# Cross attention on one core: the output product in units of 512 columns

## The chip, the core and the metric

The kernel runs on one core of one Trainium2 chip. The metric is the time of one execution on the device in microseconds, as the median of several runs. A profiled execution gives, beside its own time, the trace from which all durations here come. Engines are named as the profile names them: PE (TensorE, matmuls), PEld (its weight loads, which overlap the matmuls), DVE (VectorE), ACT (ScalarE), POOL (GpSimd) and SP (SyncE, which here only issues DMAs).

## What is computed

Thirty-two batches of 512 tokens with 640 channels attend, in 20 heads of 32 channels, to 77 keys of their own batch. The other branches of the reference see empty slices here (the context has just 77 rows), so what is left is:

```python
q = heads(x @ to_q_w)                       # x: (32, 512, 640) f32
k = heads(ctx @ to_k_w)                     # ctx: (32, 77, 1024) f32
v = heads(ctx @ to_v_w)
p = softmax(q @ k.T / sqrt(32))
out = merge(p @ v) @ to_out_w + to_out_b + x
```

All tensors are f32.

## The kernel before

**Precision.** Each f32 operand of a product is split into a high and a low part, which ACT (a cast, the high part), DVE or POOL (a subtraction, the low part) make. A product is then three matmuls: high x high, high x low, low x high (`PAIRS`).

**Stages.** A prologue makes keys and values of all batches and stores them in scratch memory. Then come 32 batches. A batch is five stages `j`, each for 128 of the 640 channels, that is four heads. A stage of number n = 5b + j has: the query product of the next stage (`queries`, L481, 15 matmuls of 512 columns into the one bank `pq`), the scores (`score_tile`, L516, four token tiles of 308 and twice 154 columns into three banks `sc`), their maximum (L527, DVE), exponentials (L541, ACT), normalisation (L556, POOL), a block transpose of the probabilities (L562, DVE) and their way through scratch memory (`pd` stores L571, `raw` loads L586 and L588, SP's queue), which turns them so that keys lie on partitions. Four stages later (`LAG`) come the value product (`value_pass`, L632, six matmuls of 512 columns into `pa`, two banks), a copy of its lower half by ACT (L646), two additions of halves by DVE (L650), and the split into `at` (L662 ACT, L667 DVE). Low parts of the queries are made by DVE (L723), those of the probabilities by DVE (L610) and POOL (L617).

**Output product.** Once a batch's five `at` tiles are there, `project` (L685) forms the output: for each of four token tiles t and two halves h of 320 channels, 15 matmuls (5 stages x 3 pairs) with `at` held and the weights `wo_s` moved, into one of two banks `po` that take turns. `add_output` (L700, DVE) adds the bank to `xr`, a tile of 128 tokens x 640 channels that SP loaded from x (L674) and to which POOL added the bias (L678); SP stores it (L703).

**Order.** Nothing is scheduled by the program's builder. The order on every engine follows three tables of tokens: `FILL` (batches 0 and 1, with the end of the prologue), `PLAN` (each of batches 2 to 30, 29 times) and `LAST_` (batch 31 and what is left). A token such as `4p8` is a stage, an operation and an argument. Those spoken of below: `q` a fifth of a query product (three matmuls), `s` a score tile, `m` its maximum, `v` one value matmul, `p` a step of the output product (three matmuls), `g` a low query half, `z` the block transpose, `A` ACT's copy of the lower half, `a` an addition of halves, `h` and `L` the split of `at`, `f` an addition of output to `xr`, `o` its store, `ur` the load of `xr`, `b` the bias. Steps of the output product for one batch are spread over the five stages of the batches after it. The last batch's output product is in tokens of its own (`Zp`, `Zf`, `Zo`).

Of the kernel before, what the change touches and what calls it, by code (L numbers as in the profile page):

```python
# [8 lines left out]
F32 = mybir.dt.float32  # L9
FPR = mybir.dt.float32r  # L10
AF = mybir.ActivationFunctionType
ALU = mybir.AluOpType
# [11 lines left out]
P = 128  # L24
Q = 32
# [26 lines left out]
def kernel(  # L52
# [25 lines left out]
    nc = tc.nc  # L78
    B, S, C = x.shape
    CA = ehs.shape[2]  # L80
    NT = B * NKEY
    NQ = S // P
# [354 lines left out]
    z = main.tile([P, NBLK, NQ, Q], F32, name="z")  # L437
    for g, (j0, nj) in enumerate(GROUPS):
        vb = main.tile([P, nj, 2, 2, P], FPR, name=f"vb{g}")
        vbs.append(vb)  # L440
# [239 lines left out]
    def output_bank(b, t, h):  # L680
        pos[b, t, h] = late[1].tile([P, S], F32, tag="po", name="po", bufs=2)

    def project(b, t, h, j):
        for m, (a, c) in enumerate(PAIRS):
            nc.tensor.matmul(  # L685
                pos[b, t, h][:, :HALF],
                ats[b * NC_ + j][:, a, t * P : (t + 1) * P],
                wos[0][:, j, c, h * HALF : (h + 1) * HALF],
                start=(j == 0 and m == 0),
                stop=(j == NC_ - 1 and m == 2),  # L690
            )

    STEPS = [(0, h, j) for h in range(2) for j in range(4)] + [(0, 0, 4), (0, 1, 4)]
    STEPS += [(t, h, j) for t in range(1, NQ) for h in range(2) for j in range(NC_)]
    CUTS = (0, 4, 8, 10, 16, 20, 24, 28, 32, 36, 40)
    def add_output(b, t, h):
        xr, cols = xrs[b, t], slice(h * HALF, (h + 1) * HALF)
        nc.vector.tensor_tensor(xr[:, cols], pos.pop((b, t, h))[:, :HALF], xr[:, cols], ALU.add)  # L700
# [8 lines left out]
    RESIDUAL = {1: (1, 0), 3: (1, 1), 4: (1, 2), 0: (2, 3)}  # L709
    BIAS = {2: (1, 0), 4: (1, 1), 0: (2, 2), 1: (2, 3)}  # L710
# [14 lines left out]
    def open_late():  # L725
# [96 lines left out]
    def issue(b, token):  # L822
# [46 lines left out]
        elif op == "p":  # L869
            t, h, c = STEPS[arg[0] if len(arg) == 1 else 10 * arg[0] + arg[1]]  # L870
            if c == 0:
                output_bank(out_b, t, h)
# [151 lines left out]
```

## Time and profile before

| | before |
|---|---|
| time, median of 3 runs (us) | 1891.99 |
| lowest and highest (us) | 1890.35, 1901.48 |
| profiled execution, its own time (us) | 1896.68 |
| its span, first to last instruction (us) | 1894.9 |
| granted TensorE clock, mean | 0.996 |

In the profile, a row of a group shows line, engine, operation, what it writes and reads, shape and count, then busy time in all and mean duration of one, then idle time of the engine just before such instructions and what ended it. A row of the windows shows the stretch, its length, and busy time (with the count of instructions) of PE, PEld, DVE, ACT and POOL, then the granted clock, the busy share of the 16 DMA engines and GB/s. A row of the chain of waits or of the timeline shows start, length (in the timeline from the first start to the last end of merged instructions) and what. A row of the waits shows who waited for whom: us in all, times, the longest.

### The profile page before, as it was taken

The page shows a single profiled execution, that of the slowest core. Times are in us where ns is not written, and L with a number is a line of the kernel's source. Part 1 is how long each engine was busy: PE and PEld are TensorE (multiplying, and loading weights), DVE is VectorE, ACT ScalarE, POOL GpSimd, SP SyncE. Part 2 cuts the span into 40 slices and gives each one's busy share as a digit, 9 for nine tenths or more (in the row PEclk, how much of TensorE's full clock was granted, in tenths as well). Part 3 has the DMA queues.
Part 4 walks back from the last instruction along what each step waited for, and adds up shares of the span by engine and source line. Part 5 has one row for each costly group of instructions (what it writes and reads, how often), then busy time and mean ns, then how long its engine had stood idle before and what let it go on. Part 6 is the DMA issues. An engine that isn't in the chain of part 4 may idle for free.

```text
span 1894.9 us, 37179 instructions
## 1 busy us (share of the span) xinstructions
PE 1864.1 (98%) x10332; PEld 1660.5 (88%) x10332; DVE 1561.0 (82%) x2494; ACT 1534.6 (81%) x6210; POOL 1363.5 (72%) x1116
## 2 busy tenths in 40 slices
PE   9999998999999999999999999999999999999998
PEld 7888896799989898899899998998899899998997
DVE  5445346999989898999999998999998999998985
ACT  3232247999989899999999998999999999998984
POOL 1100067888878888888888888888888888887874
PEclk9999999999999999999999999999999999999999
DMA  9888868989989889898999999889989899988876
GB/s 186 195 196 246 201 178 230 225 239 239 233 223 236 235 234 234 231 233 236 239 228 238 243 237 235 232 234 236 238 239 237 234 234 241 235 237 228 228 201 201
DMA packets 565020, 431.34 MB, mean 228 GB/s; under 512 B 191120, under 2 KB 473168, under 8 KB 564816
## 3 DMA queue, kind: packets, MB, share of 16 engines
q1 hardware_dynamic: 559760, 413.62, 85.2%
q0 software_dynamic: 4416, 14.34, 2.3%
q8 instruction: 85, 1.39, 0.3%
q14 instruction: 119, 0.97, 0.2%
q10 hardware_dynamic: 640, 1.02, 0.2%
HBM read 247.17 MB, written 181.64 MB: 226 GB/s over the span
## 4 chain that ended last, share of the span: by engine, by line
PE 63%; DMA 13%; SPq 5%; POOL 5%; ACT 5%; DVE 5%; issue 3%; POOLq 0%; DVEq 0%; ACTq 0%
PE pq L481 19%; PE po L685 18%; PE pa L632 7%; PE sc L516 7%; PE pv L191 6%; PE pk L191 6%; DMA raw<-pd 5%; DMA pd<-z 3%; ACT pn L541 2%; SPq L571 2%; DMA xs<-in_x_dram 2%; POOL kb L458 1%; DMA out_dram<-xr 1%; POOL xr L678 1%; DVE z L562 1%
## 5 line engine op out<-in xcount | busy, mean ns | idle before, releaser
L541 ACT ACTIVATE pn<-sc,nm 128x77 f32<-128x77 f32 x2560 | 801.1, 352 | 27.5 <-DVE nm L527 20.1
L685 PE MATMUL po<-wo_s,at 128*128 128x320 f32 x3840 | 685.9, 311 | 0.7 <-DVE at L667 0.2
L685 PEld LDWEIGHTS po<-wo_s,at 128*128 128x128 f32 x3840 | 612.8, 188 | 44.2 <-DVE xr L700 1.1
L481 PE MATMUL pq<-xt,wq_s 128*128 128x512 f32 x2400 | 627.9, 397 | 2.4 <-DVE qt L723 2.3
L541 ACT ACTIVATION_READ_ACCUMULATOR pn<-sc,nm 128x1 f32 x2560 | 587.5, 231 | 0.0
L481 PEld LDWEIGHTS pq<-xt,wq_s 128*128 128x128 f32 x2400 | 428.8, 189 | 71.5 <-issue 1.6
L556 POOL TENSOR_TENSOR pn<-pn,rs 128x1232 f32<-128x1232 f32 x160 | 388.9, 2431 | 44.5 <-DVE rs L551 42.6
L516 PEld LDWEIGHTS sc<-kb,qt 128*128 128x128 f32 x1920 | 298.7, 189 | 44.1 <-ACT pn L541 16.2
L527 DVE TENSOR_REDUCE nm<-sc 128x4 f32<-128x308 f32 x640 | 292.2, 465 | 34.5 <-PE sc L516 30.7
L516 PE MATMUL sc<-kb,qt 128*128 128x154 f32 (+1 forms) x1920 | 300.9, 277 | 14.8 <-ACT pn L541 9.6
L632 PE MATMUL pa<-pp,vb 128*128 128x512 f32 x960 | 308.9, 404 | 6.0 <-DVE at L667 4.6
L617 POOL TENSOR_TENSOR pp<-raw,pp 64x512 fp32r<-64x512 f32 x160 | 223.4, 1396 | 97.7 <-ACT pp L599 66.8
L650 DVE TENSOR_TENSOR pa<-pa,aw 64x512 f32<-64x512 f32 x320 | 222.6, 695 | 36.5 <-ACT aw L646 29.2
L562 DVE STREAM_TRANSPOSE z<-pn 128x1280 f32<-128x1280 f32 x160 | 241.6, 1510 | 12.2 <-DMA pd<-z 2.9
L719 POOL CAST qt<-qt 64x512 fp32r<-64x512 f32 x320 | 195.7, 612 | 59.3 <-ACT qt L715 45.7
L292 POOL TENSOR_TENSOR xt<-xs,xt 128x512 fp32r<-128x512 f32 x160 | 202.9, 1295 | 43.0 <-ACT xt L288 39.8
L723 DVE TENSOR_TENSOR qt<-pq,qt 64x512 fp32r<-64x512 f32 x320 | 217.4, 680 | 12.7 <-ACT qt L715 8.0
L678 POOL TENSOR_TENSOR xr<-xr,bias 128x640 f32<-128x640 f32 x128 | 202.4, 1582 | 26.8 <-DMA xr<-in_x_dram 12.3
L610 DVE TENSOR_TENSOR pp<-raw,pp 128x1024 fp32r<-128x1024 f32 x160 | 200.1, 1250 | 18.3 <-ACT pp L601 17.9
L632 PEld LDWEIGHTS pa<-pp,vb 128*128 128x128 f32 x960 | 170.4, 190 | 26.9 <-issue 4.7
L646 ACT COPY aw<-pa 64x1024 f32<-64x1024 f32 x160 | 162.2, 1014 | 31.6 <-PE pa L632 28.9
L601 ACT CAST pp<-raw 128x1024 fp32r<-128x1024 f32 x160 | 168.0, 1050 | 20.4 <-DMA raw<-pd 20.1
(48 smaller groups left out, 1617.6 us busy)
## 6 DMA issues: line engine op xcount, KB each, us to landing
pd<-z SPq DMA_DIRECT2D x640, 160.0 KB, 3.3
raw<-pd SPq DMA_DIRECT2D x160, 512.0 KB, 4.5
xs<-in_x_dram SPq DMA_DIRECT2D x128, 320.0 KB, 5.8
xr<-in_x_dram SPq DMA_DIRECT2D x128, 320.0 KB, 4.2
out_dram<-xr SPq DMA_DIRECT2D x127, 320.0 KB, 4.2
raw<-pd SPq DMA_DIRECT2D x160, 128.0 KB, 4.4
v_dram<-vs SPq DMA_DIRECT2D x80, 192.0 KB, 4.0
k_dram<-ks POOLq DMA_DIRECT2D x20, 512.0 KB, 4.5
```

The lines of the kernel that those rows point to most:

```text
L191: nc.tensor.matmul(held[j][:, :gn], w[:, k, a, :], cts[g, k][:, c, :gn], start=(k == 0 and n == 0), stop=(k == NK - 1 and n == 2),)
L481: nc.tensor.matmul(pqs[n], wq_s[:, k, a, j * P : (j + 1) * P], xts[b, k][:, c, :], start=(k == 0 and m == 0), stop=(k == NC_ - 1 and m == 2),)
L516: nc.tensor.matmul(sc[:, cols], qt[:, m, t * P : (t + 1) * P], keys_, start=(m == 0), stop=(m == 2),)
L527: nc.vector.tensor_reduce(nm, sc[:, :KCOLS].rearrange("p (h k) -> p h k", k=NKEY), AX.X, ALU.max, negate=True)
L541: nc.scalar.activation(pnb[n % 2][:, at, :NKEY], sc[:, i * NKEY : (i + 1) * NKEY], AF.Exp, bias=nm[:, i : i + 1], accum_out=sms[n][:, at : ...
L556: nc.gpsimd.tensor_tensor(pf, pf, rs.unsqueeze(2).to_broadcast([P, NQ * HPC, NKEY]), ALU.mult)
L562: nc.vector.transpose(z.rearrange("p b t j -> p t b j"), pn.rearrange("p (t h) k -> p t (h k)", t=NQ).rearrange("p t (b i) -> p t b i", i=Q),)
L617: nc.gpsimd.tensor_tensor(pp[64:, 4, :], raw[:64, 2, :], pp[:64, 4, :].bitcast(F32), ALU.subtract)
L632: nc.tensor.matmul(pas[n][:, p, :], vb[:, p, t, :], pp[:, c, :], start=(c == p), stop=(c == p + 2),)
L650: nc.vector.tensor_tensor(pa[64 * p : 64 * p + 64, 0], pa[:64, p], aw[:, p], ALU.add)
L678: nc.gpsimd.tensor_tensor(xrs[b, t], xrs[b, t], bias, ALU.add)
L685: nc.tensor.matmul(pos[b, t, h][:, :HALF], ats[b * NC_ + j][:, a, t * P : (t + 1) * P], wos[0][:, j, c, h * HALF : (h + 1) * HALF], start= ...
```

## The change

The output product of batches 0 to 30 is cut into five units of 512 columns in place of eight of 320. Units 1 to 4 are token tiles: `at` held, the first 512 channels of the weights moved, one full bank. Unit 0 is the last 128 channels for all 512 tokens, with the weights held and `at` moved, so its result has channels on partitions and tokens along the row. Sixteen transposes by DVE (`turn_output`, token `y`), each of 32 partitions x 128 elements, turn it from the bank into a tile `zt` in SBUF, from where POOL adds it to `xr` (`add_turned`, token `U`). The first 512 channels are added by DVE as before (`add_output`, token `f`). The last batch keeps the old form (`project_half`, `add_half`). The steps are numbered anew (`STEPS`), loads of `xr` and bias additions go to other stages, and all three order tables are replaced.

```diff
+    zt = main.tile([P, NQ, P], F32, name="zt")
...
-    def output_bank(b, t, h):
-        pos[b, t, h] = late[1].tile([P, S], F32, tag="po", name="po", bufs=2)
-
-    def project(b, t, h, j):
+    def output_bank(b, u):
+        pos[b, u] = late[1].tile([P, S], F32, tag="po", name="po", bufs=2)
+
+    WIDE = C - P
+
+    def project(b, u, j):
+
+        at, w = ats[b * NC_ + j], wos[0][:, j]
+        for m, (a, c) in enumerate(PAIRS):
+            if u == 0:
+                held, moved = w[:, a, WIDE:], at[:, c, :]
+            else:
+                held, moved = at[:, a, (u - 1) * P : u * P], w[:, c, :WIDE]
+            nc.tensor.matmul(
+                pos[b, u], held, moved, start=(j == 0 and m == 0), stop=(j == NC_ - 1 and m == 2)
+            )
+
+    def project_half(b, t, h, j):
...
-    STEPS = [(0, h, j) for h in range(2) for j in range(4)] + [(0, 0, 4), (0, 1, 4)]
-    STEPS += [(t, h, j) for t in range(1, NQ) for h in range(2) for j in range(NC_)]
-    CUTS = (0, 4, 8, 10, 16, 20, 24, 28, 32, 36, 40)
-    def add_output(b, t, h):
+    def turn_output(b, q, a):
+        src = pos[b, 0][q * Q : (q + 1) * Q].rearrange("p (t a j) -> p t a j", t=NQ, j=Q)
+        nc.vector.transpose(zt[a * Q : (a + 1) * Q, :, q * Q : (q + 1) * Q], src[:, :, a, :])
+
+    def add_turned(b, t):
+        xr = xrs[b, t]
+        nc.gpsimd.tensor_tensor(xr[:, WIDE:], xr[:, WIDE:], zt[:, t, :], ALU.add)
+
+    def add_output(b, t):
+        xr = xrs[b, t]
+        nc.vector.tensor_tensor(xr[:, :WIDE], pos.pop((b, 1 + t)), xr[:, :WIDE], ALU.add)
+
+
+    STEPS = [(0, j) for j in range(4)] + [(1, 0), (0, 4)] + [(1, j) for j in range(1, NC_)]
+    STEPS += [(u, j) for u in range(2, NQ + 1) for j in range(NC_)]
+
+    def add_half(b, t, h):
         xr, cols = xrs[b, t], slice(h * HALF, (h + 1) * HALF)
-        nc.vector.tensor_tensor(xr[:, cols], pos.pop((b, t, h))[:, :HALF], xr[:, cols], ALU.add)
+        nc.vector.tensor_tensor(xr[:, cols], pos.pop((b, (t, h)))[:, :HALF], xr[:, cols], ALU.add)
...
     PIECES = {3: (1, 0), 4: (1, 2), 0: (2, 4), 1: (2, 6), 2: (2, 8)}
-    RESIDUAL = {1: (1, 0), 3: (1, 1), 4: (1, 2), 0: (2, 3)}
-    BIAS = {2: (1, 0), 4: (1, 1), 0: (2, 2), 1: (2, 3)}
+    RESIDUAL = {3: (1, 0), 4: (1, 1), 0: (2, 2), 1: (2, 3)}
+    BIAS = {4: (1, 0), 0: (2, 1), 1: (2, 2), 2: (2, 3)}
...
     PLAN = (
-        "0q0 0c1 0q1 0c0 0q2 0R 0h 0l 0q3 0uk130 0q4 0L 0d0 0s0 0d1 0Q 0s1 0m0 0ux3 0p16 0r 0e0 0f10 0v0 "
...
+        "0q0 0q1 0q2 0q3 0c1 0b1 0q4 0uk130 0s0 1uv15 0p10 0r 0h 0m0 0d0 0R 0c0 0s1 0d1 0s2 0e0 0l "
...
+        "3w2 4l 4p5 3w1 4q3 4y03 4ur1 4e1 4y10 4q4 4y32 4ux0 4y20 4y00 4ux1 4K01 4v1 4y01 4Q 4p7 4y02 "
+        "4ux2 4N 4y33 4e2 4g0 4s3 4v3 4y23 4v0 4v5 4g1 4v2 4p8 4y12 4y13 4p9 4k1 4m3 4z 4k0 4v4 4A 4b0 "
+        "4w2 4e3 4a1 4w3 4y11 4K00 4w0 4y31 4y21 4y30 4w1 4y22 4a0 "
     ).split()
...
-    ADDED = {4: 1, 0: 2, 1: 2, 2: 2, 3: 2}
+    ADDED = {0: 2, 1: 2, 2: 2, 3: 2}
...
+        elif op == "y":
+            turn_output(out_b, *arg)
+        elif op == "U":
+            add_turned(b - ADDED[j], *arg)
```

More of the change, by code (lines that the diff above doesn't have):

```diff
@@ L678, in add_bias @@
         nc.gpsimd.tensor_tensor(xrs[b, t], xrs[b, t], bias, ALU.add)
-    def output_bank(b, t, h):
-        pos[b, t, h] = late[1].tile([P, S], F32, tag="po", name="po", bufs=2)
-    def project(b, t, h, j):
+    def output_bank(b, u):
[12 more added lines that the diff above has]
+    def project_half(b, t, h, j):
         for m, (a, c) in enumerate(PAIRS):
             nc.tensor.matmul(
-                pos[b, t, h][:, :HALF],
+                pos[b, (t, h)][:, :HALF],
                 ats[b * NC_ + j][:, a, t * P : (t + 1) * P],
@@ L869, in issue @@
         elif op == "p":
-            t, h, c = STEPS[arg[0] if len(arg) == 1 else 10 * arg[0] + arg[1]]
+            u, c = STEPS[arg[0] if len(arg) == 1 else 10 * arg[0] + arg[1]]
             if c == 0:
-                output_bank(out_b, t, h)
-            project(out_b, t, h, c)
+                output_bank(out_b, u)
+            project(out_b, u, c)
+        elif op == "y":
+            turn_output(out_b, *arg)
+        elif op == "U":
+            add_turned(b - ADDED[j], *arg)
         elif op == "f":
@@ L952, in final @@
                 if i < 3:
-                    pos[last, t, h] = ps.tile([P, S], F32, tag="sc", name="po", bufs=3)
+                    pos[last, (t, h)] = ps.tile([P, S], F32, tag="sc", name="po", bufs=3)
                 elif i == 3:
-                    pos[last, t, h] = ps.tile([P, S], F32, tag="pq", name="po", bufs=1)
+                    pos[last, (t, h)] = ps.tile([P, S], F32, tag="pq", name="po", bufs=1)
                 elif i < 6:
-                    output_bank(last, t, h)
+                    output_bank(last, (t, h))
                 else:
@@ L960, in final @@
                         pas[N] = late[1].tile([P, 2, S], F32, tag="pa", name="po", bufs=1)
-                    pos[last, t, h] = pas[N][:, i - 6]
-            project(last, t, h, j)
+                    pos[last, (t, h)] = pas[N][:, i - 6]
+            project_half(last, t, h, j)
         elif op == "f":
-            add_output(last, *arg)
+            add_half(last, *arg)
         elif op == "o":
```

150 rows, old and new, of tables (FILL, LAST_, PLAN) are left out of this document.

## Prediction

> **What bounds the kernel now.** I read the page's totals first, then the windows by stage, then the chain of waits inside one batch, then the waits of PE and DVE.
>
> ```profile
> PE 1864.1 (98%) x10332; PEld 1660.5 (88%) x10332; DVE 1561.0 (82%) x2494; ACT 1534.6 (81%) x6210; POOL 1363.5 (72%) x1116
> ```
> ```profile
> core 0: us, PE busy (x) PEld busy (x) DVE busy (x) ACT busy (x) POOL busy (x), PEclk, DMA share, GB/s
> 0.00:340.00 340.00, 324.62 (x1471) 274.18 (x1472) 172.80 (x275) 134.01 (x404) 90.45 (x106) 0.98 0.86 206
> ...
> 1002.31:1494.30 491.99, 490.60 (x2826) 442.27 (x2826) 446.91 (x716) 451.75 (x1885) 410.98 (x327) 1.00 0.90 236
> 1800.00:1895.00 95.00, 88.86 (x528) 80.29 (x527) 69.71 (x111) 61.93 (x236) 55.98 (x42) 1.00 0.68 200
> ```
> The averages of the page mix a prologue, in which DVE is half idle, with the batches. The third row is ten steady batches: 491.99 us, so 49.2 us a batch. There PE is busy 490.60, ACT 451.75 (92%) and DVE 446.91 (91%, 44.7 us a batch). PE sets the pace, but two engines follow close behind it.
>
> A busy PE is not a PE at its best, so the next view is the chain of waits through one batch, where a piece's length over its matmul count is the spacing from start to start:
>
> ```profile
> 1002.31 3.49 PE pq L481 x15
> ...
> 1007.93 0.70 PE pa L632 x3
> ...
> 1009.23 2.63 PE po L685 x18
> 1011.86 3.43 PE pq L481 x15
> 1015.29 0.69 PE sc L516 x6
> ...
> 1051.51 3.49 PE pq L481 x15
> ```
> The reader is to see two things. The same piece comes back after 1051.51 - 1002.31 = 49.20 us: one period. And spacing goes with columns: 3.43/15 to 3.49/15 = 229 to 233 ns for 512 columns, 2.63/18 = 146 ns for 320. The group rows give 311 ns for the 320-column matmul, but that counts its fill and drain, which the next one overlaps; whoever counts with durations finds a large gain that isn't there. A batch by spacings: 75 query matmuls at 231, 120 output matmuls at 146, 30 value matmuls at 233 and 20 score tiles at 0.345 us make 17.33 + 17.53 + 7.0 + 6.9 = 48.8 us. Only some 0.4 us of the 49.2 is waiting.
>
> ```profile
> PEld sc L516 <- ACT pn L541: 6.2, 12, 1.1
> PEld pa L632 <- DVE at L667: 2.5, 9, 0.3
> ```
> These are the largest waits ahead of PE between 600 and 1700 us, 22 batches: 0.4 us a batch, the same answer from the other side.
>
> **Output product on PE.** Before, 4 token tiles x 2 halves x 15 = 120 matmuls of 320 columns; after, 5 units x 15 = 75 matmuls of 512. The columns are the same, 38,400. At 146 ns the old ones take 17.53 us a batch. At 229 to 233 ns the new ones take 17.15 to 17.45, middle 17.30. Saved: 0.23 us a batch, ends 0.08 and 0.38. It applies to batches 0 to 30, as the last batch keeps its halves: 31 x 0.23 = 7 us (2.5 to 12), and it counts in full because PE is the pace. The 45 weight loads that go lay beside matmuls and give nothing more. Swapping which operand is held changes nothing in these spacings: query matmuls already hold weights and move activations.
>
> [...]
>
> **DVE.** Eight adds of 320 become four of 512, and 16 transposes of 32 x 128 from PSUM come in.
>
> ```profile
> L700 DVE TENSOR_TENSOR xr<-po,xr 128x320 f32<-128x320 f32 x256 | 120.7, 473 | 8.4 <-PE po L685 5.4 <-POOL xr L678 0.2
> L278 DVE STREAM_TRANSPOSE xs<-xs 128x640 f32<-128x640 f32 x128 | 100.0, 817 | 4.7 <-DMA xs<-in_x_dram 4.6
> L167 DVE STREAM_TRANSPOSE craw<-cs 128x512 f32<-128x512 f32 x32 | 21.6, 696 | 7.6 <-DMA cs<-in_ctx_dram 7.3
> L254 DVE STREAM_TRANSPOSE vs<-pv 128x512 f32<-128x512 f32 x20 | 14.2, 710 | 15.5 <-DMA v_dram<-vs 13.3 <-PE pv L191 2.2
> ```
> ```profile
> 1002.87 0.84 DVE L527 TENSOR_REDUCE nm<-sc 128x4 f32<-128x308 f32 x2
> ...
> 1005.84 0.24 DVE L551 RECIPROCAL rs<-sm 128x16 f32<-128x16 f32 x1
> 1006.00 1.16 DVE L610 TENSOR_TENSOR pp<-raw,pp 128x1024 fp32r<-128x1024 f32 x1
> ...
> 1026.11 1.56 DVE L278 STREAM_TRANSPOSE xs<-xs 128x640 f32<-128x640 f32 x2
> ...
> 1029.76 1.51 DVE L562 STREAM_TRANSPOSE z<-pn 128x1280 f32<-128x1280 f32 x1
> 1031.20 0.21 DVE L551 RECIPROCAL rs<-sm 128x16 f32<-128x16 f32 x1
> ...
> 1035.82 0.68 DVE L667 TENSOR_TENSOR at<-pa,at 128x512 fp32r<-128x512 f32 x1
> 1036.42 1.56 DVE L278 STREAM_TRANSPOSE xs<-xs 128x640 f32<-128x640 f32 x2
> ...
> 1043.57 0.47 DVE L700 TENSOR_TENSOR xr<-po,xr 128x320 f32<-128x320 f32 x1
> 1043.97 0.46 DVE L527 TENSOR_REDUCE nm<-sc 128x4 f32<-128x308 f32 x1
> ```
> On DVE too the next instruction starts before the last has ended, so I price by starts. An add of 320 costs 1043.97 - 1043.57 = 0.40, one of 512 costs 0.60 (the L667 row, also PSUM with SBUF): 8 x 0.40 - 4 x 0.60 = 0.8 us a batch saved. Transposes: 1.44 for 1280 (1029.76 to 1031.20), 1.56 - 0.82 = 0.74 for 640, so 1.09 ns an element, and 0.74 - 512 x 1.09 ns = 0.18 for 128. From PSUM it is 14 ns more (710 against 696). No row shows so small a transpose, and none of 32 partitions. Its lower bound is 0.16, the 16-element reciprocal (1005.84 to 1006.00); its upper one the whole duration with nothing overlapped, 710 - 384 x 1.09 = 0.29. I take 0.20, from the transposes, the nearest rows in kind: 3.2 us a batch (2.6 to 4.6). DVE goes from 44.7 to 44.7 - 0.8 + 3.2 = 47.1 us of a 49.0 us period (46.5 to 48.5). I cost this at nothing because PE still has more to do; if that cover goes, it is rival B.
>
> [...]
>
> **Where the transposes stand.** They follow step p5, which ends unit 0, in stage 4 of the table. Behind them on DVE wait the two query halves (g), a score maximum (m3), the block transpose (z) and the half adds (a1, a0). Unit 2 (p10, next batch) needs unit 0's bank, so it waits for the last transpose. From the end of p5 PE has 6 query matmuls, 9 of units 0 and 1, 6 value matmuls and a score tile (21 x 0.232 + 0.35 = 5.2 us), then 15 query matmuls and a tile (3.8): 9.0 us.
>
> ```profile
> L646 ACT COPY aw<-pa 64x1024 f32<-64x1024 f32 x160 | 162.2, 1014 | 31.6 <-PE pa L632 28.9
> ```
> DVE passes 11 transposes, g0, g1, m3 and z in 2.2 + 1.2 + 0.4 + 1.4 = 5.2 us; a1 must wait for the last value matmul and ACT's copy of 1.01, at 6.4; then a1 and the five last transposes end at 8.0. That leaves 1.0 us; at 0.29 each it is still 0.5. So p10 isn't late. The maximum m0 of the next batch needs its tile at 9.0, after a0 (8.6). ACT gets nothing new.
>
> **POOL and the queues.** The table adds four 128 x 128 additions a batch.
>
> ```profile
> L678 POOL TENSOR_TENSOR xr<-xr,bias 128x640 f32<-128x640 f32 x128 | 202.4, 1582 | 26.8 <-DMA xr<-in_x_dram 12.3 <-issue 4.6 <-DMA kb<-k_dram 2.7
> L292 POOL TENSOR_TENSOR xt<-xs,xt 128x512 fp32r<-128x512 f32 x160 | 202.9, 1295 | 43.0 <-ACT xt L288 39.8
> ```
> 1582 - 512 x 2.24 = 0.44 us each, 1.7 us a batch (nothing to 5.2, at L292's price): POOL goes from 41.1 to 42.8 of 49; nobody else gains or loses by it. The output store on SP now waits for POOL's addition too, and pd stores and raw loads stand behind it; the table puts each addition ahead of its store by a stage in three tiles, and by half a stage in the last. Residual loads move later by one or two stages, bias additions go with them; DMA bytes and issues are unchanged. All priced at nothing.
>
> **Order tables.** All three are new. In the steady part an order can win at most the 0.4 us a batch of waiting. In the prologue PE idles 340 - 324.6 = 15.4 us, much of it before any token of the table, and at the end 6.1. I take zero, plus or minus 5.
>
> **Sum.** The profiled execution took 1896.7 us for a span of 1894.9; minus 7 it is 1889.7. It stood 4.7 above the median, so the forecast against the median is 1892 - 7 = 1885.
>
> **Rivals.**
> A, PE stays the pace, 1885 (1875 to 1895).
>
> B, slower: DVE becomes the pace. For it: 47.1 of 49.0 leaves 1.9 us idle where there were 4.5, and idle here is mostly answers of other engines:
>
> ```profile
> DVE at L667 <- ACT at L662: 40.1, 51, 1.1
> DVE nm L527 <- PE sc L516: 19.2, 43, 0.6
> DVE pa L650 <- ACT aw L646: 14.2, 51, 0.7
> DVE pp L610 <- ACT pp L601: 10.3, 15, 1.7
> ```
> That is 83.8 us over 22 batches, 3.8 a batch, in loops that a longer DVE queue hides only in part. It decides once transposes and remaining idle pass 49.0 - 43.9 = 5.1 us: at 0.20 each, if over 1.9 us of idle stays. With 3.0 staying the batch is 43.9 + 3.2 + 3.0 = 50.1, +0.9 x 30 = 27 us: 1919. [...] Against it: the walk above, where each loop keeps half a microsecond.
>
> C, the new order also removes waits: 0.4 x 29 = 12 us and 5 at the ends on top of A: 1868. Against it: a fuller DVE makes waits, it doesn't remove them.
>
> D, nothing: the spacing goes strictly with columns and saves 0.08 a batch: 1890.
>
> **How the numbers follow.** A 0.55, D 0.13, C 0.08, B 0.24. One per cent, 19 us, is about what a measurement of this kernel can tell from no change: under 1873 only C lies, 0.08 faster; A and D are the same, 0.68; B is slower, 0.24. The likeliest is A: 1885. The range takes in most of C (1869) and the milder half of B (1920).
>
> **What would show it.** In the profile after: 512-column output matmuls in the chain at 229 to 233 ns; PE near 490 of 492 us in ten batches, and a period of 49.0; the transposes near 0.27 us long and 0.20 from start to start; DVE near 96%. If instead PE waits before po for a transpose, or sc and pa for DVE, and the period passes 49.6, B has it. If DVE sits under 93%, a transpose is cheaper than I think. A time under 1869 would mean that 512 columns run closer than the query matmuls do.

## The result, and the profile after

| | before | after |
|---|---|---|
| median of 20 runs (us) | 1896.01 | 1901.81 |
| lowest and highest (us) | 1888.68, 1905.08 | 1899.28, 1906.82 |
| profiled execution, its own time (us) | 1896.68 | 1900.52 |
| its span (us) | 1894.9 | 1898.7 |

The ratio of after to before is 1.0032, 95% interval 1.0018 to 1.0045. That is within the one per cent that the prediction calls the same, and 1901.8 lies inside its range. But the change lost 6 us where the forecast had it win 7: the range held the time only because it was drawn up to 1920 to take in some of rival B. The kernel before is itself 4 us slower here than in the three runs that the forecast counted from.

First the totals of the page of the kernel after:

```profile
PE 1859.1 (98%) x8937; PEld 1551.9 (82%) x8937; DVE 1666.5 (88%) x2866; ACT 1526.2 (80%) x6210; POOL 1387.1 (73%) x1240
```

Then the windows, 600 to 1600 us, of before and of after:

```profile
core 0: us, PE busy (x) PEld busy (x) DVE busy (x) ACT busy (x) POOL busy (x), PEclk, DMA share, GB/s
600.00:1600.00 1000.00, 996.91 (x5744) 899.08 (x5744) 905.74 (x1451) 919.36 (x3833) 837.48 (x667) 1.00 0.90 236
```
```profile
600.00:1600.00 1000.00, 988.96 (x4813) 824.94 (x4812) 968.14 (x1685) 908.38 (x3811) 847.46 (x743) 1.00 0.90 234
```

A batch has 285 matmuls before and 240 after (45 went). So the stretch holds 5744/285 = 20.15 batches before, 49.62 us each, and 4813/240 = 20.05 after, 49.86 each. DVE has gone from 905.74/20.15 = 44.9 to 48.3 us a batch, and PE, which was idle for 3.1 us of the 1000, is idle for 11.0. The reader sees there that PE now waits, but not for whom. The waits of after between 600 and 1700 us, 22 batches, say it:

```profile
PEld po L694 <- PE sc L517: 13.8, 22, 0.7
...
PE po L694 <- DVE zt L710: 11.1, 22, 0.6
DVE pa L651 <- ACT aw L647: 10.4, 22, 0.5
...
DVE at L668 <- ACT at L663: 2.9, 7, 1.2
...
DVE nm L528 <- PE sc L517: 0.2, 1, 0.2
```

One wait of PE stands out: `po` for `zt`, the transposes, 22 times in 22 batches, 11.1/22 = 0.50 us each. DVE's own waits, 40.1 + 19.2 + 14.2 + 10.3 us before, have shrunk to 10.4 + 2.9 + 0.2, and the fourth, for `pp`, is gone: DVE's queue is nearly always late. The groups of the whole run give the sizes of the new work:

```profile
L694 PE MATMUL po<-wo_s,at 128*128 128x512 f32 x1860 | 510.9, 399 | 15.5 <-DVE zt L710 15.5
...
L710 DVE STREAM_TRANSPOSE zt<-po 32x128 f32<-32x128 f32 x496 | 155.0, 312 | 11.0 <-PE po L694 2.7
...
L714 POOL TENSOR_TENSOR xr<-xr,zt 128x128 f32<-128x128 f32 x124 | 59.3, 478 | 7.4
```

A transpose lasts 0.312 us, and 155.0/31 = 5.0 us a batch are spent on them. Where that lands is seen in one batch. The timelines of after, PE first, then DVE (start, length, instructions; merged where equal ones follow each other):

```profile
1007.13 0.86 PE L694 MATMUL po<-at,wo_s 128*128 128x512 f32 x3
1007.83 1.55 PE L482 MATMUL pq<-xt,wq_s 128*128 128x512 f32 x6
...
1010.14 0.49 PE L517 MATMUL sc<-kb,qt 128*128 128x308 f32 x3
1010.47 1.14 PE L633 MATMUL pa<-pp,vb 128*128 128x512 f32 x4
...
1013.07 3.59 PE L482 MATMUL pq<-xt,wq_s 128*128 128x512 f32 x15
1016.50 0.48 PE L517 MATMUL sc<-kb,qt 128*128 128x308 f32 x3
1017.46 0.93 PE L694 MATMUL po<-wo_s,at 128*128 128x512 f32 x3 [0.48 <-DVE zt L710]
```
```profile
1008.02 2.59 DVE L710 STREAM_TRANSPOSE zt<-po 32x128 f32<-32x128 f32 x8
1010.62 0.68 DVE L749 TENSOR_TENSOR qt<-pq,qt 64x512 fp32r<-64x512 f32 x1
1011.32 0.32 DVE L710 STREAM_TRANSPOSE zt<-po 32x128 f32<-32x128 f32 x1
1011.65 0.69 DVE L749 TENSOR_TENSOR qt<-pq,qt 64x512 fp32r<-64x512 f32 x1
1012.38 0.64 DVE L710 STREAM_TRANSPOSE zt<-po 32x128 f32<-32x128 f32 x2
1013.04 0.48 DVE L528 TENSOR_REDUCE nm<-sc 128x4 f32<-128x308 f32 x1
1013.55 1.51 DVE L563 STREAM_TRANSPOSE z<-pn 128x1280 f32<-128x1280 f32 x1
1014.99 0.67 DVE L651 TENSOR_TENSOR pa<-pa,aw 64x512 f32<-64x512 f32 x1
1015.69 1.63 DVE L710 STREAM_TRANSPOSE zt<-po 32x128 f32<-32x128 f32 x5
1017.35 0.69 DVE L651 TENSOR_TENSOR pa<-pa,aw 64x512 f32<-64x512 f32 x1
```

This is the walk of the prediction. Step p5 is the first row, ended at 1007.99. PE's work up to p10 ends at 1016.98, so it is 9.0 us, as forecast. DVE's stretch, forecast at 8.0, runs from 1008.02 to 1015.69 + 1.63 = 1017.32, 9.3 us. The slack of 1.0 became a lack of 0.3, and with some 0.15 from the last transpose to the first matmul that is the gap of 0.48. The gap is counted from the end of the score matmul; p10 follows the score tile by 0.96 where another piece follows one by 0.33 (1010.47 - 1010.14), so 0.63 us of PE are lost.

None of the first eight transposes overlaps the next: 2.59 us for eight is (2.59 - 0.31)/7 = 0.326 from start to start, a duration and 14 ns. The long `z` does overlap what follows it (1013.55 to 1014.99 is 1.44, its duration 1.51).

### The profile page after: what moved, and what is told of

It reads as the page before. It is cut to its first block, busy times and chain, and to the rows that moved or that the text cites. A ratio compares the mean times of both kernels' runs of the same rounds, so it can differ in the third digit from the quotient of the medians.

```text
span 1898.7 us, 35065 instructions
## 1 busy us (share of the span) xinstructions
PE 1859.1 (98%) x8937; PEld 1551.9 (82%) x8937; DVE 1666.5 (88%) x2866; ACT 1526.2 (80%) x6210; POOL 1387.1 (73%) x1240
## 3 DMA queue, kind: packets, MB, share of 16 engines
q8 instruction: 74, 1.21, 0.3%
## 5 line engine op out<-in xcount | busy, mean ns | idle before, releaser
L482 PE MATMUL pq<-xt,wq_s 128*128 128x512 f32 x2400 | 640.9, 397 | 4.0 <-DVE qt L749 3.0
L542 ACT ACTIVATION_READ_ACCUMULATOR pn<-sc,nm 128x1 f32 x2560 | 563.8, 220 | 0.0
L694 PE MATMUL po<-wo_s,at 128*128 128x512 f32 x1860 | 510.9, 399 | 15.5 <-DVE zt L710 15.5
L482 PEld LDWEIGHTS pq<-xt,wq_s 128*128 128x128 f32 x2400 | 443.0, 189 | 97.6 <-ACT pn L542 3.2
L694 PEld LDWEIGHTS po<-wo_s,at 128*128 128x128 f32 x1860 | 331.2, 189 | 79.7 <-PE sc L517 17.7
L557 POOL TENSOR_TENSOR pn<-pn,rs 128x1232 f32<-128x1232 f32 x160 | 364.2, 2276 | 28.0 <-DVE rs L552 18.2
L517 PEld LDWEIGHTS sc<-kb,qt 128*128 128x128 f32 x1920 | 319.1, 189 | 57.2 <-ACT pn L542 5.8
L618 POOL TENSOR_TENSOR pp<-raw,pp 64x512 fp32r<-64x512 f32 x160 | 233.2, 1457 | 119.5 <-DVE nm L528 58.5
L633 PE MATMUL pa<-pp,vb 128*128 128x512 f32 x960 | 287.4, 402 | 5.1 <-DVE at L668 4.0
L745 POOL CAST qt<-qt 64x512 fp32r<-64x512 f32 x320 | 211.9, 662 | 77.0 <-ACT qt L741 63.5
L611 DVE TENSOR_TENSOR pp<-raw,pp 128x1024 fp32r<-128x1024 f32 x160 | 193.7, 1211 | 1.4 <-ACT pp L602 1.4
```

The source lines that it names most:

```text
L482: nc.tensor.matmul(pqs[n], wq_s[:, k, a, j * P : (j + 1) * P], xts[b, k][:, c, :], start=(k == 0 and m == 0), stop=(k == NC_ - 1 and m == 2),)
L517: nc.tensor.matmul(sc[:, cols], qt[:, m, t * P : (t + 1) * P], keys_, start=(m == 0), stop=(m == 2),)
L542: nc.scalar.activation(pnb[n % 2][:, at, :NKEY], sc[:, i * NKEY : (i + 1) * NKEY], AF.Exp, bias=nm[:, i : i + 1], accum_out=sms[n][:, at : ...
L557: nc.gpsimd.tensor_tensor(pf, pf, rs.unsqueeze(2).to_broadcast([P, NQ * HPC, NKEY]), ALU.mult)
L618: nc.gpsimd.tensor_tensor(pp[64:, 4, :], raw[:64, 2, :], pp[:64, 4, :].bitcast(F32), ALU.subtract)
L633: nc.tensor.matmul(pas[n][:, p, :], vb[:, p, t, :], pp[:, c, :], start=(c == p), stop=(c == p + 2),)
```

## The experiments

Each kernel is the one after with the edit shown; the medians stand beside 1893 to 1894 of the kernel before on the same chips.

**No transposes.** The transposes are left out, and with them the product's part in the last 128 channels; POOL adds zeros.

```diff
-        src = pos[b, 0][q * Q : (q + 1) * Q].rearrange("p (t a j) -> p t a j", t=NQ, j=Q)
-        nc.vector.transpose(zt[a * Q : (a + 1) * Q, :, q * Q : (q + 1) * Q], src[:, :, a, :])
+        return
```


> The changed kernel without its 16 transposes a batch: the last 128 output channels get no product. Theory T (the transposes cost DVE 0.325 us each from start to start, 5.2 us a batch, so that DVE is busy 97% and unit 0's bank comes free too late): without them DVE falls to about 43.5 us a batch (87%), the wait of po for zt is gone, the steady period falls from 49.7 to 48.9-49.2 us, and the ratio to the kernel before is 0.988 to 0.996. Rival O (the new order tables, not the transposes, hold PE): the period stays at 49.5 or more and the ratio at 1.000 to 1.004.

1880.90 us, ratio 0.9932 (0.9919 to 0.9945), and no wait of PE for DVE is listed but three at `pa`, 1.8 us in all. So the loss lies in the transposes: all else that the change did wins 0.7%.

**One transpose.** A single transpose of 128 x 512 in each 32 x 32 block, in place of sixteen of 32 x 128; the blocks stay in their 32 partitions, so the last 128 channels are permuted.

```diff
+        if b not in turned:
+            turned.append(b)
+            nc.vector.transpose(zt.rearrange("p t c -> p (t c)"), pos[b, 0])
```


> One transpose of 128 x 512 in place of the 16 of 32 x 128: the same elements are turned, but each 32 x 32 block stays in its own quarter of the partitions, so the blocks of the last 128 output channels stand in the wrong places. Theory T, count and not elements cost: about 0.6 us of DVE a batch, period 48.9-49.3, ratio 0.990 to 0.997, within 0.002 of the run without transposes. Rival O: period 49.5 or more, ratio 1.000 to 1.004. Rival E (reading the bank costs by elements): nearer to the changed kernel than to the run without transposes.

1879.89 us, 0.9925 (0.9912 to 0.9938). One instruction of 0.72 us is free.

**Sixteen in one group of partitions.** As many transposes, of the same shape, at the same places of the order; but all read partitions 0 to 31 of the bank and write partitions 0 to 31 of `zt`, so most of the last 128 channels are left out of the output.

```diff
+        src = pos[b, 0][:Q].rearrange("p (t a j) -> p t a j", t=NQ, j=Q)
+        n = turns.setdefault(b, [0])
+        nc.vector.transpose(zt[:Q, :, n[0] % 4 * Q : (n[0] % 4 + 1) * Q], src[:, :, a, :])
```


> The same 16 transposes of 32 x 128 in the same places of the order, but all from partitions 0-31 to partitions 0-31, so the last 128 output channels are wrong. Theory Q (a transpose is held until the one before has ended because its input or output starts in another quarter of the partitions): from start to start 0.18 to 0.24 us in place of 0.325, that is 1.4 to 2.3 us of DVE a batch less, and the ratio to the kernel before falls to 0.990 to 0.999. Rival S (a small transpose costs 0.32 whatever its partitions): 0.32 from start to start, ratio 1.001 to 1.005.

1880.47 us, 0.9926 (0.9915 to 0.9938): as fast as without them. From the timeline of DVE of this kernel, and its windows:

```profile
1046.15 1.69 DVE L713 STREAM_TRANSPOSE zt<-po 32x128 f32<-32x128 f32 x8 [0.20 <-PE po L696]
...
1053.11 1.08 DVE L713 STREAM_TRANSPOSE zt<-po 32x128 f32<-32x128 f32 x5
```
```profile
600.00:1600.00 1000.00, 998.97 (x4878) 834.94 (x4877) 950.38 (x1714) 919.47 (x3857) 861.54 (x752) 1.00 0.90 237
```

Eight take 1.69 where they took 2.59, five 1.08 where they took 1.63. One starts 0.198 us after another, and lasts 0.26. So neither the count nor the shape nor reading from the bank makes them dear, but that the input or the output of each starts in another group of 32 partitions than that of the one before it. PE is busy 998.97 of 1000 again.

**Only the input fixed; only the output fixed.** The two halves of the last edit alone, one run each.

```diff
-        src = pos[b, 0][q * Q : (q + 1) * Q].rearrange("p (t a j) -> p t a j", t=NQ, j=Q)
+        src = pos[b, 0][:Q].rearrange("p (t a j) -> p t a j", t=NQ, j=Q)
```


> The 16 transposes with their own output quarter, but all reading partitions 0-31 (the last 128 output channels are wrong). Theory Q (held when input or output starts in another quarter than in the instruction before): held, 0.325 us from start to start, except where two neighbours write the same quarter: one pair of the first eight, two of the last five, so the first eight take 2.4 to 2.5 us in place of 2.6 and the last five 1.35 to 1.4 in place of 1.63. If only the input's quarter counts: 0.20 throughout, the first eight 1.65 to 1.75 us.

```diff
-        nc.vector.transpose(zt[a * Q : (a + 1) * Q, :, q * Q : (q + 1) * Q], src[:, :, a, :])
+        n = turns.setdefault(b, [0])
+        nc.vector.transpose(zt[:Q, :, n[0] % 4 * Q : (n[0] % 4 + 1) * Q], src[:, :, a, :])
```


> The 16 transposes with their own input quarter, but all writing partitions 0-31 (the last 128 output channels are wrong). Theory Q: held, 0.325 us, except where two neighbours read the same quarter: two pairs of the first eight, none of the last five, so the first eight take 2.3 to 2.4 us in place of 2.6 and the last five 1.6. If only the output's quarter counts: 0.20 throughout, the first eight 1.65 to 1.75 us.

1888.93 and 1896.40 us. The first eight and the last five transposes of a batch, in the timeline of the kernel with the input fixed:

```profile
1004.08 2.42 DVE L710 STREAM_TRANSPOSE zt<-po 32x128 f32<-32x128 f32 x8 [0.21 <-PE po L694]
...
1011.57 1.34 DVE L710 STREAM_TRANSPOSE zt<-po 32x128 f32<-32x128 f32 x5
```

and with the output fixed:

```profile
1005.67 2.41 DVE L713 STREAM_TRANSPOSE zt<-po 32x128 f32<-32x128 f32 x8
...
1013.08 1.69 DVE L713 STREAM_TRANSPOSE zt<-po 32x128 f32<-32x128 f32 x5
```

With the input fixed, the last five are y11 y31 y21 y30 y22 and write groups 1, 1, 1, 0, 2: the spacing is 0.198 from the second to the third, 0.24 from the first to the second, and 0.28 and 0.32 where the group changes. With the output fixed they read 1, 3, 2, 3, 2, and every spacing is 0.34 to 0.35. Either side alone, input or output, is enough to hold an instruction. How far the stretch shrinks, from the start of the row of eight to the end of the row of five, decides the wait behind it. The period here is the time between starts of the reciprocal of stage 4, from the trace, batch after batch.

| kernel | stretch in one batch (us) | PE's listed wait for `zt`, a batch (us) | most common period (us) | time (us) |
|---|---|---|---|---|
| after | 1017.32 - 1008.02 = 9.30 | 11.1/22 = 0.50 | 49.71 | 1901.81 |
| output fixed | 1014.77 - 1005.67 = 9.10 | 6.4/22 = 0.29 | 49.54 | 1896.40 (one run) |
| input fixed | 1012.91 - 1004.08 = 8.83 | none | 49.27 | 1888.93 (one run) |
| both fixed | 1054.19 - 1046.15 = 8.04 | none | 49.05 | 1880.47 |

With the input fixed no wait for `zt` is listed, but PE's rows of that batch show a short one:

```profile
1012.56 0.48 PE L517 MATMUL sc<-kb,qt 128*128 128x308 f32 x3
1013.06 0.93 PE L694 MATMUL po<-wo_s,at 128*128 128x512 f32 x3
```

p10 follows the score tile by 0.50 us where 0.33 is enough, and it starts 0.15 behind the last transpose, as in after. Against the 49.05 of both fixed, the periods are longer by 0.22, 0.49 and 0.66 us at stretches of 8.83, 9.10 and 9.30: what the stretch has over some 8.6 us is added to the period. That point is close to PE's 9.0 us less the 0.15 of the hand-over and the 0.15 by which a piece may start before the score tile's end.

**Transposes earlier.** If the last five only came too late for p10, then moving them up would do. First ahead of the block transpose `z`:

```diff
-        "4ux2 4N 4y33 4e2 4g0 4s3 4v3 4y23 4v0 4v5 4g1 4v2 4p8 4y12 4y13 4p9 4k1 4m3 4z 4k0 4v4 4A 4b0 "
-        "4w2 4e3 4a1 4w3 4y11 4K00 4w0 4y31 4y21 4y30 4w1 4y22 4a0 "
+        "4ux2 4N 4y33 4e2 4g0 4s3 4v3 4y23 4v0 4v5 4g1 4v2 4p8 4y12 4y13 4p9 4k1 4m3 4y11 4y31 4y21 4y30 "
+        "4y22 4z 4k0 4v4 4A 4b0 4w2 4e3 4a1 4w3 4K00 4w0 4w1 4a0 "
```


> In the steady table alone, the last five transposes of a batch go ahead of the block transpose z; nothing else is changed. Theory K (PE is held by the late release of unit 0's bank, 0.5 us a batch): the bank is free some 2 us earlier, the wait of po for zt is gone, the period falls by up to 0.5 us, ratio 0.993 to 0.999. Rival C (DVE's whole load sets the period, and PE's wait only shows where): PE waits as long at another tile that DVE releases, period 49.6 to 49.8, ratio 1.001 to 1.005.

1918.13 us, 1.0127 (1.0114 to 1.0140): worse by far. Its waits, 600 to 1700 us:

```profile
POOL kb L459 <- DMA kb<-k_dram: 39.5, 22, 2.4
...
PE pa L633 <- DVE at L668: 10.6, 24, 0.5
```

The wait of `po` is gone, and as long a one has come at the value product, which waits for the split of `at` behind the half adds. Beside it POOL waits for the load of keys, 39.5 us against 11.6 in after, and the weight loads of the value product wait 27.7 against 2.6, released by "issue", that is by nothing which the trace shows. A later `z` makes its stores later, and SP issues them ahead of the key loads in one queue; that this is the road was argued, not tried alone.

Then between `z` and the half adds, so that `z` keeps its place:

```diff
-        "4w2 4e3 4a1 4w3 4y11 4K00 4w0 4y31 4y21 4y30 4w1 4y22 4a0 "
+        "4w2 4e3 4y11 4y31 4y21 4y30 4y22 4a1 4w3 4K00 4w0 4w1 4a0 "
```


> In the steady table alone, the last five transposes of a batch go ahead of the half add a1 and stay behind the block transpose z, so nothing of z and of the pd stores behind it on SP's queue moves. Theory K (the changed kernel loses its time where PE waits for unit 0's bank, 0.5 us a batch): the bank is free 0.7 us earlier, the wait of po for zt is gone, the period falls from 49.7 to 49.1-49.3, ratio to the kernel before 0.992 to 0.998. Rival C (DVE's load as such, 97%, sets the period): PE waits as long for another DVE result, period 49.6 or more, ratio 1.000 to 1.005.

1905.28 us, 1.0064 (1.0051 to 1.0078). From its waits:

```profile
PEld pa L633 <- issue: 22.9, 29, 1.0
...
PE pa L633 <- DVE at L668: 11.3, 25, 0.6
```

The 11.1 us at `po` have become 11.3 at `pa`, and the weight loads there wait for nothing that the trace names, as in the run before. This reads as if no place of the transposes were late by itself: DVE has more work than time from p5 to the next split of `at`, and the wait stands at the first thing behind it. The runs with less work on DVE test that.

**Turned through memory.** One transpose as above, then four stores to scratch memory and one load, which put the blocks in their places; the whole computation.

```diff
+        if n[0] == 0:
+            nc.vector.transpose(zt.rearrange("p t c -> p (t c)"), pos[b, 0])
+        elif 4 <= n[0] < 8:
+            r = slice((n[0] - 4) * Q, (n[0] - 3) * Q)
+            nc.sync.dma_start(
+                zds[b].rearrange("(g j) c -> j g c", j=Q)[:, :, r],
+                zt[r].rearrange("j t c -> j (t c)").rearrange("j (g i) -> j g i", i=Q),
+            )
+        elif n[0] == 15:
+            nc.sync.dma_start(zt, zds[b].rearrange("(t p) c -> p t c", p=P))
```


> The whole computation, with one transpose of 128 x 512 a batch on DVE in place of 16; the blocks change their quarter of the partitions on the way out to scratch memory (four stores with runs of 128 bytes) and back (one load). Theory T: DVE near 90%, no wait of po for zt, period 49.05 to 49.3, ratio 0.992 to 0.998, as in the run with one transpose, if the transfers are hidden. Rival M (DMA engines at 90% and SP's queue can't take five more transfers a batch): stores and loads of probabilities land later, PE waits for pa or sc, period 49.6 or more, ratio 1.000 to 1.010.

1940.80 us, 1.0250 (1.0229 to 1.0270). Its waits, and its DMA issues (count, KB each, us from issue to landing):

```profile
POOL kb L460 <- DMA kb<-k_dram: 54.3, 20, 3.6
ACT pp L603 <- DMA raw<-pd: 39.1, 21, 2.9
...
PE sc L518 <- ACT pn L543: 16.9, 19, 1.7
```
```profile
zd<-zt SPq DMA_DIRECT2D x124, 64.0 KB, 5.3
zt<-zd SPq DMA_DIRECT2D x31, 256.0 KB, 3.3
```

DVE is down to 871.93 us busy in the window of 1000, and yet this is the slowest of all, far over the 1.010 at which the rival's range ended. With five more transfers a batch, 4 x 64 + 256 KB, beside DMA engines that were 0.90 busy, the loads come late on which ACT and POOL wait. Whether the engines' load did it, or the new issues ahead of those loads in SP's queue, was not separated.

**Work taken off DVE.** If DVE's stretch is too long, then less work in it must remove the wait wherever it stands. One of the five subtractions of a batch that make the low parts of the probabilities (L611, 1.21 us) is the next on DVE behind this stretch; it is given to POOL, with the transposes between `z` and the half adds.

```diff
-        nc.vector.tensor_tensor(
+        engine = nc.gpsimd if n % NC_ == 1 and NC_ * 2 < n < NC_ * 30 else nc.vector
+        engine.tensor_tensor(
```


> As the run with the last five transposes ahead of a1, and in stage 0 of the batches POOL, not DVE, makes the low part of the probabilities (128 x 1024, 1.13 us of DVE a batch; by POOL's 1.29 us for 128 x 512 some 2.5 us of POOL's). Theory L (between the start of the transposes and the split of at in the next stage 0 DVE has more to do than PE, and nothing but less DVE work there helps): both waits, po for zt and pa for at, are gone, the period falls from 49.77 to 49.05-49.3, ratio to the kernel before 0.993 to 0.999. Rival P (POOL at 86% can't take 2.5 us more): the value product waits for POOL, period 49.5 or more, ratio 1.000 to 1.010.

1897.56 us, 1.0025 (1.0013 to 1.0037). From its waits:

```profile
PEld sc L517 <- POOL qt L746: 7.0, 22, 0.4
...
PE sc L517 <- POOL qt L746: 2.1, 11, 0.2
...
PE pa L634 <- DVE at L669: 0.4, 1, 0.4
```

The wait at `pa` is gone (11.3 to 0.4) and none is listed at `po`; against its order alone that is 0.4%. But the score tile now waits for POOL's query half: POOL takes 2.40 us for the subtraction where DVE took 1.21.

The same edit of the engine in the order of after, where the wait stands ahead of that subtraction:

> The changed kernel in its own order, with the same low part on POOL. Theory L: that work stands behind the transposes on DVE, so it can't free unit 0's bank earlier: PE waits on for zt, 0.4 to 0.5 us a batch, period 49.5 to 49.75, ratio 1.000 to 1.004. Rival C (DVE's load as such sets the period): with 1.13 us less the wait is gone, period 49.05 to 49.3, ratio 0.993 to 0.999.

1902.69 us, 1.0047 (1.0034 to 1.0059). From its waits:

```profile
PE po L695 <- DVE zt L711: 10.9, 22, 0.6
```

Nothing is gained: what is taken away behind the wait doesn't shorten the way to it.

Half of the subtraction on POOL, half on DVE, again with the transposes between `z` and the half adds:

```diff
+        if n % NC_ == 1 and NC_ * 2 < n < NC_ * 30:
+            for engine, r in ((nc.vector, 0), (nc.gpsimd, 1)):
+                engine.tensor_tensor(
+                    pp[:, 2 + r, :], raw[:, r, :], pp[:, r, :].bitcast(F32), ALU.subtract
+                )
```


> As the run with the last five transposes ahead of a1 and the low part of the probabilities in stage 0 on POOL, but only half of it (128 x 512) goes to POOL: 0.5 us of DVE a batch less ahead of the split of at, where PE waited 0.47, and 1.3 us more on POOL in place of 2.5. Theory L: the wait of pa for at shrinks to under 0.1 us a batch, that of sc for POOL's query copies (0.36 with the whole on POOL) does too, period 49.05 to 49.3, ratio to the kernel before 0.993 to 0.999, under that of the kernel before. Rival W (every order of this table has a wait of that size somewhere on DVE or POOL): period 49.4 or more, ratio 1.001 to 1.005.

1895.38 us, 1.0013 (1.0002 to 1.0024), not the gain over the kernel before that was expected. PE is busy 998.79 us of 1000 and waits 1.0 us for `at` in 22 batches, but the most common period is 49.45, not 49.05. The missing 0.4 us are spread: beside sixteen in one group, a batch has 0.13 us more between score matmuls, 0.16 behind score tiles and 0.09 ahead of the value product, by the starts of the matmuls. The value product's weight loads wait 10.8 us in 22 batches, released by "issue" again. So the numbers that rival W had came; that every order of this table keeps such a wait, as it says, isn't shown. It is the best version with the whole computation, and it doesn't beat the kernel before.

**The split first.** With the transposes between `z` and the half adds, the low part of `at` is moved ahead of that subtraction (all of it on DVE again), which itself goes behind seven more tokens.

```diff
-        "0q0 0q1 0q2 0q3 0c1 0b1 0q4 0uk130 0s0 1uv15 0p10 0r 0h 0m0 0d0 0R 0c0 0s1 0d1 0s2 0e0 0l "
-        "0uk100 0p11 0m1 0ur2 0L 0p12 0Q 1uv10 0m2 0e1 0p13 0uk110 0f0 0N 1d0 0v1 0s3 0g1 1d1 0e2 0v3 "
+        "0q0 0q1 0q2 0q3 0c1 0b1 0q4 0uk130 0s0 1uv15 0p10 0r 0h 0m0 0d0 0L 0c0 0s1 0d1 0s2 0e0 0l "
+        "0uk100 0R 0p11 0m1 0ur2 0p12 0Q 1uv10 0m2 0e1 0p13 0uk110 0f0 0N 1d0 0v1 0s3 0g1 1d1 0e2 0v3 "
```


> As the run with the last five transposes ahead of a1, and in stage 0 of the steady table the split of at (L) goes ahead of the low part of the probabilities (R); the work of each engine is unchanged. Theory O2 (the order is at fault, DVE has room): the wait of pa for at is gone and none takes its place, period 49.05 to 49.3, ratio 0.993 to 0.999. Theory L: the wait moves on to the next value matmuls or score tiles, period 49.6 or more, ratio 1.001 to 1.008.

1925.05 us, 1.0167 (1.0153 to 1.0182). From its waits:

```profile
PE pa L633 <- POOL pp L618: 14.5, 22, 0.7
...
PE sc L517 <- POOL qt L745: 5.1, 22, 0.2
```

The wait has moved once more, to the next value product, and one is added. But it isn't the order alone: POOL's own subtraction (L618) now starts together with DVE's, and takes longer.

```profile
1031.06 1.22 DVE L611 TENSOR_TENSOR pp<-raw,pp 128x1024 fp32r<-128x1024 f32 x1
1031.06 2.34 POOL L618 TENSOR_TENSOR pp<-raw,pp 64x512 fp32r<-64x512 f32 x1 [2.32 <-DVE nm L528]
```

In the same place it takes 1.62 us where 0.48 us of DVE's subtraction lie beside it (the run with the transposes between `z` and the half adds alone), and 1.30 where that subtraction is POOL's. DVE's takes 1.2 either way.

**Against what was expected.** The runs that change the hold itself came out as its theory said, to 0.1 us in a row of the timeline. Of the orders, and of the way through memory, the ratios (1.0127, 1.0064, 1.0167, 1.0250) lie above even the ranges for the slower case. With less work on DVE and the transposes ahead of the half adds the wait for it went, but the most common period stayed at 49.45, not 49.05 to 49.3. So the hold is shown to be the cause of the loss; that DVE's stretch is all that stands in the way of a gain is not.

## Why the prediction was wrong

**The step that failed** is the price of a transpose: "I take 0.20, from the transposes, the nearest rows in kind: 3.2 us a batch (2.6 to 4.6)". It measured 0.326 from start to start, 16 x 0.326 = 5.2 us, above the upper bound of 0.29 too. The rows that it was taken from had the whole 128 partitions, so each started in the same group as its neighbour; these sixteen are all different pairs of an input group and an output group, and no two in a row agree in both. The same instruction with the same partitions took 0.198, so 0.20 was the right price of what the rows could show, and the mistake was to take it for another case. With the price failed the step that rested on it, "I cost this at nothing because PE still has more to do": the hold cost PE 0.66 us a batch, some 20 us in all. The upper bound "with nothing overlapped" was the right idea, but its duration was too short: a held transpose lasts 0.312, one that isn't 0.26.

The trace of before had the sign of it. Its DVE timeline has this row, not far behind those that the prediction quotes:

```profile
1017.06 1.39 DVE L723 TENSOR_TENSOR qt<-pq,qt 64x512 fp32r<-64x512 f32 x2
```

Two of 0.68 us in 1.39 don't overlap at all, where the two transposes of 0.82 at L278, quoted for the price, take 1.56 and so overlap by 0.08. The two that don't overlap lie in different halves of the partitions.

By the runs the price of the hold is the whole duration of the instruction before and 14 ns, 0.312 + 0.014 = 0.326. The two runs with one side fixed show that each side counts: where the output alone changed its group, 0.28 and 0.32 us from start to start, where the input alone did, 0.34 to 0.35, and 0.198 where neither did. Sixteen transposes of the same size in one group cost 16 x 0.198 = 3.2 us, the very sum of the forecast.

**The walk** was right in its frame: unit 0's bank was named as the place, PE's 9.0 us were 9.0, and nearly all by which the stretch passed it goes back to the price. "At 0.29 each it is still 0.5" didn't hold: DVE took 9.3, of which 11 x 0.126 = 1.4 come ahead of a1 and 5 x 0.126 = 0.6 behind it, less the wait of 1.2 for ACT's copy that a1 no longer has. That makes 8.8, and most of the rest is that the work between them overlapped nothing either: from start to start a query half took 0.70 us, a half add 0.70 and the maximum 0.51, at durations of 0.68, 0.67 and 0.48, where the walk had 0.6, 0.6 and 0.4. The slack too was smaller than its 1.0 us: without a loss the stretch may last 8.6, not 9.0.

**Rival B** was to decide once transposes and remaining idle pass 5.1 us, and the transposes alone are 5.2. So B has it by its own test (a period of 49.86, over 49.6; PE waits ahead of `po` for a transpose), though mildly: 1901.8, not 1919, since DVE is the pace in one stretch of the batch only and idles 1.6 us in the rest. "DVE near 96%" came out 97%.

**PE's saving.** The 512-column matmuls are 232 ns apart, inside the 229 to 233 of the forecast. Each lasts 399 ns, and one of 320 columns, 146 apart, 311: the 167 and 165 ns by which they outlast the spacing are what the prediction calls fill and drain, and the next matmul overlaps them. The commonest period falls from 49.20 to 49.05 (sixteen in one group): 0.15 saved, inside 0.08 to 0.38, below the 0.23 taken. That this is the columns alone was not tried, as the order tables changed with them.

**The period and the order tables.** "Ten steady batches" was a misreading: the row had x2826 matmuls, 2826/285 = 9.92 batches, so 49.6 us each. The chain showed one batch of 49.20, but the trace of before has several of 50 to 52.7, and its mean is 0.5 us above its commonest. "In the steady part an order can win at most the 0.4 us" was therefore too low, and zero not the likeliest. Counted by the reciprocals of stage 4, over 30 batches of one profiled execution each:

```
                           common   mean   ends (first mark + what follows the last)
before                     49.20    49.72  319.1 + 84.3 = 403.4
after                      49.71    49.84  322.9 + 80.5 = 403.4
sixteen in one group       49.05    49.11  322.4 + 80.8 = 403.2
```

The ends came out at nothing, as taken. A batch of after against one of before: -0.15 for the columns, +0.66 for the hold (49.71 - 49.05), and -0.39 for late batches that no longer come (0.52 over the commonest before, 0.13 after). The sum, +0.12, times 30 is 3.6 us of the 3.8 between the spans. So rival C was half right: it took 0.4 x 29 = 12 us of waits away, and 0.39 x 30 = 12 went, but nothing at the ends. Without the hold the change would have been at 0.9926, which is 1878 against the forecast's 1892, between A's 1885 and C's 1868. That the order tables, and not the units, removed the late batches was not separated.

**DVE's adds and POOL.** No term of the small ones decided. Without transposes DVE is busy 882.11 us in 1000, x4865 on PE or 20.27 batches: 43.5 us against 44.9 before, 1.4 less where 0.8 was taken. The additions' own durations, 0.473 us for 320 columns and 0.662 for 512, give 8 x 0.473 - 4 x 0.662 = 1.1 of it. An addition on POOL took 0.478, not 0.44.

How much the hold costs in all: 1.0032 - 0.9926 = 1.06%, 20 us, which ate a gain of 14 and left a loss of 6.

## What to carry to other kernels

Price an instruction by rows in which the instruction in front of it is in the same relation to it as it will be in the new place: same partitions, or not. Sixteen small transposes that changed their partitions every time paid a full duration each here, 0.326 us from start to start against 0.198; order such instructions, or choose their inputs and outputs, so that runs of them start in the same group on both sides, where the data allows it. Here it doesn't: the sixteen are sixteen different pairs of groups, so in any order each differs from its neighbour on one side at least. And when moving work on an engine moves a wait and leaves its length (11.1, 11.3, 10.6 us here), suspect that the engine has more work than time in that stretch, and take work away to see.

## What the runs showed of the hardware

- Between two DVE transposes of 32 x 128 with nothing to wait for, start to start was 0.198 us where input and output started in the same 32 partitions as before (0.24 after the first of a row). It was the full duration and 14 ns (0.326) in the kernel after, where one or both change every time, 0.34 to 0.35 where the input alone changed, and 0.28 and 0.32 where the output alone did. The instruction itself was shorter too in one group, 0.26 against 0.312.
- Five transposes of 0.33 us moved ahead of `z` took the ratio from 1.0032 to 1.0127, though the largest of PE's named waits stayed at 10.6 us; with them behind `z` and ahead of the half adds it was 1.0064. That the later stores and loads behind `z` are the reason is argued, not shown.
- Half a megabyte a batch of extra transfers, at 0.90 busy DMA engines, cost 2.5% while they freed DVE: the busy share rose only to 0.92, and the price appeared at other loads, which engines awaited for up to 3.6 us. The engines' load and the new issues in SP's queue were not separated.
- A subtraction of 64x512 on POOL lasted 1.49, 1.62, 1.82 and 2.34 us where 0.34, 0.48, 0.67 and 1.21 us of DVE's subtraction of 128x1024, begun before it or with it, lay beside it, whose inputs are both in SBUF. It stayed at 1.29 beside 0.65 us of a subtraction that reads a bank (L668), and in before where POOL's began first: there DVE's lasted 1.32, 1.82 and 2.35 us beside 0.24, 0.74 and 1.27 of POOL's, against a median of 1.22.
